# Attention: long products in half-bank pieces, one or two beside every block

## The chip, the cores and the metric

The kernel runs on one core of one Trainium2 chip. The metric is the device time of one execution in microseconds, the median of several runs. Engines are named as in the profile: PE (TensorE's matmuls) and PEld (its weight loads), DVE (VectorE), ACT (ScalarE), POOL (GpSimd), SP (the queue that issues most transfers).

## The reference

A layer of three parts on x of shape (8, 512, 512), all in float32:

```python
x = x + 0.5 * ffn(layernorm(x))      # 16 experts choose 256 tokens each; one shared expert matrix
x = x + attention(layernorm(x))
x = x + 0.5 * ffn(layernorm(x))
```

The attention is a differential one, and the change lies in it. For each of 16 heads (4 groups of keys and values, head width 32) there are two causal softmax maps, and the second is taken away from the first with a factor; the difference goes through a softmax of its own:

```python
q = rope((x @ Wq).reshape(b, s, H, 2 * D))
k = rope((x @ Wk).reshape(b, s, KVH, 2 * D))
v = (x @ Wv).reshape(b, s, KVH, D)
scores = softmax(where(causal, NEG, energy) / sqrt(D))
diff = softmax(where(causal, NEG, scores[:, 0] - lam * scores[:, 1]))
att = einsum("bhqv,bvhd->bqhd", diff, v)
att = att * rsqrt(mean(att * att, -1) + EPS) * rms_w * (1 - LAM_INIT)
return att.reshape(b, s, E) @ Wo
```

## The kernel before

The order of the instructions is written out by hand. The first feed-forward part runs over the 8 batches, then attention, then the second feed-forward part.

**Blocks.** Attention is a list of 176 blocks, 22 for each batch. A batch has two phases (`gp` 0 and 1: two of the four key groups each), so there are 16 phases of 11 blocks. A phase goes over the four query tiles `i` of 128 queries: one block for tile 0, two for tile 1, four each for tiles 2 and 3, the later tiles with more keys. The main loop takes one block `k` further in each turn, and in the same turn works on earlier blocks, so that every engine has a stage of a different block:

- PE: transposes of the probabilities of block k-3 (`turn_pe`, L882), attention sums of block k-4 (`values_pe`, L913), short products, and the scores of the next block (`scores`, L761), which go into PSUM banks 0 to 3;
- DVE: the reciprocals of block k-1 (L799), then the "first subtraction" of block k (`energies`, L777: mask and minimum, 4, 8 or 16 operations that read banks 0 to 3), then the slot "mid", copies of the transposes (L898) and of the attention sum (L926), the slot "dve", and the difference of the two maps of block k-1 (L848);
- ACT: exponentials of an earlier block's difference (L862), exponentials of block k (L790), the slots "act first", "act mid" and "act", copies of the transposes (L900);
- POOL: masks (L828), factors and weights (L804, L814), and the slot "pool".

**Work in slots.** What belongs to no block stands beside blocks, in named slots filled by a table: `rope_steps` (a projection of q or k, L635, its two rotation products on DVE, L654 and L656, two transfers on SP's queue that swap neighbouring rows, and a sum on POOL, L665), `value_steps` (L610), `norm_steps` (statistics on DVE, normalising on POOL, transposes on PE, L582, and a copy to `hT` on ACT, L589) and `finish_steps` (the normalisation of the attention sum, with short products L694, L700 and L715, a multiplication L723, the output projection L731 and the residual L737). There are ten projections of q and k, four output projections and one of the values in each batch. In a phase's turns from 0 to 10 the projections stand at (0, 0, 1, 2, 3) or (0, 1, 1, 2, 4), each as a whole: four products of 512 columns into one PSUM bank, two of the products in the slot "long" and two in "long 2".

**The next scores.** A table says where the scores of the next block stand in the turn: ahead of "long" (0), between "long" and "long 2" (1), or behind both (2):

```python
PLACES = (1, 0, 1, 2, 2, 0, 0, 0, 0, 0, 2, 0, 0, 0, 0, 0, 0, 0, 0, 0, 0, 0)
```

**Banks.** PSUM has eight banks of 512 float32 columns. Banks 0 to 3 hold scores, 4 and 5 the transposes. Banks 6 and 7 (`MISC`) are taken in turn by everything else, long or short: projections, attention sums, transposes of the normalised x, the products of `finish_steps`. A tile is waited for by the tile that takes its bank next.

Of the kernel before, what the change touches and what calls it, by code (L numbers as in the profile page):

```python
# [23 lines left out]
Q = P // 2  # L24
NEXP = 16
# [16 lines left out]
def macaron_kernel(  # L42
# [80 lines left out]
    turns = {}  # L123

    def bank(of, name, shape=(P, S)):

        n = turns[of] = turns.get(of, -1) + 1
        return banks.tile(list(shape), F32, name=name, tag=f"b{of[n % len(of)]}")
# [414 lines left out]
    def attention(f0, f1, home, first_end, projections_end, drain):  # L543
        QSCALE = -1.0 / float(D) ** 0.5

        def misc(name):
            return bank(MISC, name)


        def norm_steps(at, b, st):  # L550

            mv = tiny.tile([P, TPB, 2], F32, name=f"mv{b}", tag="a_mv", bufs=1)
            rstd = tiny.tile([P, TPB], F32, name=f"rstd{b}", tag="a_rstd", bufs=1)
            nmr = tiny.tile([P, TPB], F32, name=f"nmr{b}", tag="a_nmr", bufs=1)
            hs, ps = {}, {}

            def stats(i):
                s6 = tiny.tile([P, 6], F32, name=f"s6_{b}_{i}", tag="a_s6")
                nc.vector.bn_stats(s6, x_sb[b][:, i, :])
                nc.vector.bn_aggr(mv[:, i, :], s6)  # L560

            def scale():
                nc.scalar.activation(rstd, mv[:, :, 1], AF.Ln, bias=ln_eps)
                nc.scalar.activation(rstd, rstd, AF.Exp, scale=-0.5)

            def shift():
                nc.vector.scalar_tensor_tensor(
                    nmr, mv[:, :, 0], -1.0, rstd, ALU.mult, ALU.mult
                )

            def apply(i):
                where, tag = home["h"]
                hs[i] = where.tile([P, E], F32, name=f"h{b}_{i}", tag=tag, bufs=2)
                return nc.gpsimd.tensor_scalar(
                    hs[i], x_sb[b][:, i, :], rstd[:, i : i + 1], nmr[:, i : i + 1],
                    ALU.mult, ALU.add,
                )

            def turn(i):
                ps[i] = misc(f"htp{b}_{i}")  # L580
                for c in range(EC):
                    nc.tensor.transpose(  # L582
                        ps[i][:, c * P : (c + 1) * P], hs[i][:, c * P : (c + 1) * P], ident
                    )

            def put(i):
                if i == 0:
                    st["hT"] = home["hT"].tile([P, EC, S], F32, name=f"hT{b}", tag="hT")
                nc.scalar.copy(  # L589
                    st["hT"][:, :, i * P : (i + 1) * P],  # L590
                    ps[i].rearrange("p (c t) -> p c t", c=EC),
                )

            for i in range(TPB):
                at((0, 0, 3, 3)[i], "dve", lambda i=i: stats(i))
                at((6, 6, 8, 9)[i], "pool", lambda i=i: apply(i))
                at((7, 8, 9, 10)[i], "short", lambda i=i: turn(i))
                at((7, 8, 9, 10)[i], "act mid", lambda i=i: put(i))
            at(3, "act", scale)
            at(4, "mid", shift)  # L600

        def value_steps(at, o, b, st):
            t = {}

            def pe(h):
                if h == 0:
                    t["ps"] = misc(f"vps{b}")
                for i in (2 * h, 2 * h + 1):
                    for c in range(EC):
                        nc.tensor.matmul(  # L610
                            t["ps"][:, i * P : (i + 1) * P],
                            st["hT"][:, c, i * P : (i + 1) * P], wv_sb[:, c, :],
                            start=(c == 0), stop=(c == EC - 1),
                        )

            def act():
                st["v"] = home["v"].tile([P, TPB, KVH * D], F32, name=f"v{b}", tag="v", bufs=2)
                nc.scalar.copy(st["v"].rearrange("p i d -> p (i d)"), t["ps"])

            at(o, "long", lambda: pe(0))  # L620
            at(o, "long 2", lambda: pe(1))
            at(o + 1, "act first", act)

        def rope_steps(at, o, b, gp, n, st):

            name = f"r{b}_{gp}_{n}"
            c0 = gp * P if n == 0 else (gp * R + n - 1) * P
            w = wk_sb if n == 0 else wq_sb
            t = {}

            def pe(h):
                if h == 0:
                    t["ps"] = misc(f"{name}_ps")
                for c in (2 * h, 2 * h + 1):
                    nc.tensor.matmul(  # L635
                        t["ps"], w[:, c, c0 : c0 + P], st["hT"][:, c, :],
                        start=(c == 0), stop=(c == EC - 1),
                    )

            def place():  # L640

                tiles, tag = st["kq"][gp], f"kq{gp}_"
                if n == 0:
                    tiles["k"] = home[f"kq{gp}"].tile([P, S], F32, name=name, tag=f"{tag}k")
                    return tiles["k"]
                h, r = divmod(n - 1, 2)
                if h == 0:
                    tiles[r] = home[f"kq{gp}"].tile([P, S, 2], F32, name=name, tag=f"{tag}{r}")
                return tiles[r][:, :, h]

            def dve():
                f = 1.0 if n == 0 else QSCALE
                out = t["out"] = place()
                nc.vector.scalar_tensor_tensor(out, t["ps"], f, cosk, ALU.mult, ALU.mult)  # L654
                by = home["by"].tile([P, S], F32, name=f"{name}_by", tag="by", bufs=2)
                nc.vector.scalar_tensor_tensor(by, t["ps"], -f, sink, ALU.mult, ALU.mult)  # L656

                t["sw"] = home["sw"].tile([P, S], F32, name=f"{name}_sw", tag="sw", bufs=2)
# [8 lines left out]
            at(o, "long", lambda: pe(0))  # L667
            at(o, "long 2", lambda: pe(1))
            at(o + 1, "mid", dve)
            at(o + 2, "pool", pool)  # L670

        def finish_steps(at, os, b, i, st):
# [4 lines left out]
            def square():  # L677
                t["sq"] = home["sq"].tile([P, 4, P], F32, name=f"{name}_sq", tag="sq", bufs=2)
# [10 lines left out]
            def sums():  # L689


                t["ss"] = misc(f"{name}_ss")
# [17 lines left out]
            def turn():  # L710

                t["f"] = misc(f"{name}_f")
                for c in range(4):
                    for q in range(4):
                        nc.tensor.matmul(  # L715
                            t["f"][q * D : (q + 1) * D, c * P : (c + 1) * P],
# [4 lines left out]
            def norm():  # L721
                t["an"] = home["sq"].tile([P, 4, P], F32, name=f"{name}_an", tag="sq", bufs=2)
                nc.vector.tensor_tensor(  # L723
                    t["an"], st["aT"][i], t["f"].rearrange("p (c q) -> p c q", c=4), ALU.mult
                )
# [13 lines left out]
            o0, o1, o2, o3, o4 = os  # L739
            at(o0, "act", square)  # L740
            at(o1, "short", sums)
            at(o1, "act mid", root)
            at(o3, "short", turn)
            at(o3, "dve", norm)
            at(o4, "long", lambda: pe(0))
            at(o4, "long 2", lambda: pe(1))
            at(o4 + 1, "mid", residual)
# [154 lines left out]
        def values_pe(u):  # L902
# [3 lines left out]
            av = misc(f"av{u['id']}")  # L906
            u["av"] = av
# [77 lines left out]

        def plan(ph):
# [3 lines left out]
            if gp == 0:  # L990
                if b < B:
                    for n, o in enumerate((0, 0, 1, 2, 3)):
                        rope_steps(at, o, b, 1, n, sts[b])
                    if b + 1 < B:
                        sts[b + 1] = new_batch()
                        norm_steps(at, b + 1, sts[b + 1])
                if b > 0:
                    finish_steps(at, (0, 1, 2, 4, 5) if b < B else LAST[0], b - 1, 2, sts[b - 1])
                    finish_steps(at, (3, 5, 5, 7, 8) if b < B else LAST[1], b - 1, 3, sts[b - 1])
            else:  # L1000
                if b + 1 < B:
                    for n, o in enumerate((0, 1, 1, 2, 4)):
                        rope_steps(at, o, b + 1, 0, n, sts[b + 1])
                    value_steps(at, 3, b + 1, sts[b + 1])
                finish_steps(at, (4, 5, 5, 7, 9), b, 0, sts[b])
                finish_steps(at, (6, 7, 7, 9, 10), b, 1, sts[b])
                if b == B - 1:
                    for n, os in enumerate(EARLY):
                        early_steps(at, n, *os)

# [25 lines left out]
        order = ("short", "long", "long 2", "act mid", "mid", "dve", "act", "pool")  # L1036
        pre = placer(-20)
        norm_steps(pre, 0, sts[0])
        for n in range(R + 1):
            rope_steps(pre, 12 + n, 0, 0, n, sts[0])  # L1040
# [15 lines left out]
        value_steps(placer(-2), 0, 0, sts[0])  # L1056
# [11 lines left out]
        for k in range(K + 13):  # L1068
            u = blocks[k] if k < K else None
            u1, uE, u2, u3 = (blocks[k - d] if 0 <= k - d < K else None for d in (1, 2, 3, 4))  # L1070
            if k in starts:
                ph = starts.index(k)
                if ph == 2 * B - 1:
# [23 lines left out]
            place = PLACES[k % len(PLACES)]  # L1097
# [94 lines left out]
    for i in range(TPB):  # L1192
# [5 lines left out]
        hT=proj, kq0=proj, by=proj, sw=proj, h=(proj, "sw")  # L1198
# [3 lines left out]
    def first_end():  # L1202
        first_y.close()
        opened["out"], opened["blocks"] = pool("out", "right"), pool("blocks", "right")
        home.update(aT=opened["out"], sq=opened["out"], h=(opened["out"], "sq"))
# [51 lines left out]

    attention(f0, f1, home, first_end, projections_end, drain)
# [13 lines left out]
    for name in ("late", "out", "early"):  # L1272
        opened[name].close()

# [68 lines left out]
```

## Time and profile before

| what | before |
|---|---|
| median of 3 runs | 1421.35 us (1421.13 to 1421.44) |
| profiled execution, first to last instruction | 1420.2 us |
| mean granted clock of TensorE | 0.969 |
| busy: PE, DVE, ACT, POOL | 1328.5, 1154.9, 1047.0, 685.4 us |
| one batch of attention, in the steady part | 129.6 us |
| projections of q (L635, wq) | 512 passes of 601 ns |
| first subtraction (L777) | 1024 operations of 453 ns |
| rotation (L654, L656) | 80 each, 690 and 681 ns |
| swap transfers | 160 of 128 KB, 2.0 us to landing |

The page's first part gives the busy time of each engine and its share of the span, the second the same in 40 slices of 35.5 us, in tenths. A matmul in float32 stands in the trace as two passes. A group's mean is the length of one instruction; instructions that follow each other on an engine overlap by a part of it, so that their spacing is shorter than their length.

### The profile page before, as it was taken

How to read it: one execution, taken by the hardware profiler on the slowest of the kernel's cores; microseconds unless marked ns; L12 is line 12 of the kernel's file. 1: busy time of each engine (PE TensorE's matmuls, PEld its weight loads, DVE VectorE, ACT ScalarE, POOL GpSimd, SP SyncE). 2: the span in 40 equal slices, each digit the busy share in tenths (PEclk: the TensorE clock that was granted, in tenths of full speed). 3: DMA queues.
4: the chain of work that ended last, by engine and by line, in shares of the span. 5: the costliest groups of instructions: out<-in, count | busy, mean ns of one | idle time of the engine just before them, and what ended most of it. 6: DMA issues, size and time to landing. Idle time of an engine off the chain costs nothing.

```text
span 1420.2 us, 30675 instructions
## 1 busy us (share of the span) xinstructions
PE 1328.5 (94%) x9774; PEld 738.4 (52%) x9774; DVE 1154.9 (81%) x4405; ACT 1047.0 (74%) x3644; POOL 685.4 (48%) x1314
## 2 busy tenths in 40 slices
PE   6999899899999999999999999999999997998998
PEld 4544444455555555555555555555455555555443
DVE  6554769899989988998999899889989989654566
ACT  3411128999899898989898998989899989844110
POOL 5433626554555455454545555554545555443230
PEclk9999988999999999999999999999999997999999
DMA  9300011000000101000000001010000001000006
GB/s 344 91 1 0 0 38 38 9 31 24 16 24 17 39 1 38 9 31 9 32 24 16 28 13 39 2 38 16 24 13 27 28 13 40 1 5 1 1 1 236
DMA packets 27554, 48.19 MB, mean 34 GB/s; under 512 B 4720, under 2 KB 6016, under 8 KB 27392
## 3 DMA queue, kind: packets, MB, share of 16 engines
q1 hardware_dynamic: 25152, 42.03, 8.3%
q10 hardware_dynamic: 2208, 4.19, 0.8%
q8 instruction: 77, 1.26, 0.4%
q14 instruction: 85, 0.70, 0.2%
q0 software_dynamic: 32, 0.01, 0.0%
HBM read 16.86 MB, written 8.39 MB: 18 GB/s over the span
## 4 chain that ended last, share of the span: by engine, by line
PE 60%; ACT 13%; DVE 10%; issue 2%; POOL 0%; ACTq 0%; DVEq 0%
PE r_ps L635 18%; PE sc L761 8%; PE f_o L731 8%; ACT e L790 7%; PE tp L882 6%; PE yps L381 6%; PE av L913 4%; DVE e L777 4%; DVE t L848 3%; ACT t L862 2%; PE vps L610 2%; PE kps L403 2%; PE f_f L715 1%; ACT eT L900 1%; PE tp L325 1%
## 5 line engine op out<-in xcount | busy, mean ns | idle before, releaser
L790 ACT ACTIVATE e<-e,nb 128x192 f32<-128x192 f32 (+7 forms) x1024 | 535.5, 532 | 6.5 <-DVE nb L777 4.3
L777 DVE CUSTOM_DVE_ANT_0 e<-sc,mpos 128x192 f32<-128x192 f32 (+7 forms) x1024 | 400.8, 453 | 23.7 <-PE sc L761 16.5
L814 POOL TENSOR_SCALAR e<-e,z 128x512 f32<-128x512 f32 (+7 forms) x512 | 295.9, 590 | 16.7
L862 ACT ACTIVATE t<-t,nm 128x512 f32<-128x512 f32 (+7 forms) x512 | 270.0, 534 | 42.2 <-DVE nm L848 42.0
L761 PE MATMUL sc<-r,r 32*128 32x64 f32 (+7 forms) x2048 | 245.3, 456 | 10.8 <-DVE nb L777 4.9
L848 DVE CUSTOM_DVE_ANT_0 t<-e,z 128x512 f32<-128x512 f32 (+7 forms) x512 | 240.6, 518 | 5.1 <-POOL e L814 4.2
L635 PE MATMUL r_ps<-hT,wq_sb 128*128 128x512 f32 x512 | 235.6, 601 | 0.1
L381 PE MATMUL yps<-we,y 128*128 128x512 f32 x456 | 216.5, 612 | 1.0 <-ACT y L388 0.7
L882 PEld LDWEIGHTS tp<-ident,t 128*128 128x128 f32 x1280 | 146.5, 144 | 135.6 <-ACT eT L900 43.3
L882 PE MATMUL tp<-ident,t 128*128 128x128 f32 x1280 | 188.6, 283 | 28.1 <-ACT eT L900 26.6
L790 ACT ACTIVATION_READ_ACCUMULATOR e<-e,nb 128x1 f32 x1024 | 202.1, 197 | 0.0
L665 POOL TENSOR_TENSOR r<-r,r_sw 128x512 f32<-128x512 f32 x80 | 103.0, 1296 | 175.8 <-DVE z L799 84.2
L761 PEld LDWEIGHTS sc<-r,r 32*128 32x128 f32 x2048 | 117.4, 188 | 90.7 <-DVE nb L777 44.6
L391 POOL TENSOR_TENSOR y<-y,eb 128x512 f32<-128x512 f32 x57 | 73.1, 1283 | 164.4 <-ACT y L388 134.3
L635 PEld LDWEIGHTS r_ps<-hT,wq_sb 128*128 128x128 f32 x512 | 93.0, 190 | 113.9 <-issue 99.6
L388 ACT COPY y<-yps 128x512 f32<-128x512 f32 x57 | 33.4, 586 | 155.6 <-PE yps L381 155.6
L828 POOL TENSOR_SCALAR_AFFINE_SELECT e<-e 128x128 f32<-128x128 f32 x256 | 79.2, 316 | 99.4 <-ACT e L790 99.4
L898 DVE COPY eT<-tp 128x512 f32<-128x512 f32 (+1 forms) x176 | 112.0, 636 | 16.6 <-PE tp L882 16.6
L381 PEld LDWEIGHTS yps<-we,y 128*128 128x128 f32 x456 | 81.3, 192 | 78.4 <-issue 73.6
L731 PE MATMUL f_o<-wo_sb,f_an 128*128 128x512 f32 x256 | 118.6, 605 | 0.0
L804 POOL TENSOR_TENSOR z<-z,over 128x4 f32<-128x4 f32 (+1 forms) x192 | 38.0, 201 | 142.6 <-DVE z L799 142.5
L862 ACT ACTIVATION_READ_ACCUMULATOR t<-t,nm 128x1 f32 x512 | 100.4, 196 | 0.0
(123 smaller groups left out, 1668.6 us busy)
## 6 DMA issues: line engine op xcount, KB each, us to landing
r_sw<-r_by SPq DMA_DIRECT2D x160, 128.0 KB, 2.0
x<-in_x_dram SPq DMA_DIRECT2D x6, 1024.0 KB, 13.2
out_dram<-x SPq DMA_DIRECT2D x6, 512.0 KB, 3.2
out_dram<-x ACTq DMA_DIRECT2D x6, 512.0 KB, 3.2
x<-in_x_dram SPq DMA_DIRECT2D x8, 256.0 KB, 8.2
we<-in_expert_w_dram SPq DMA_DIRECT2D x2, 1024.0 KB, 7.7
wq_sb<-in_wq_dram SPq DMA_DIRECT2D x1, 2048.0 KB, 13.9
wo_sb<-in_wo_dram SPq DMA_DIRECT2D x8, 128.0 KB, 2.8
```

The source lines that it names most:

```text
L381: nc.tensor.matmul(held["yps"], buf[b][:, i, c * P : (c + 1) * P], held["we"][:, c, :], start=(c == 0), stop=(c == EC - 1),)
L635: nc.tensor.matmul(t["ps"], w[:, c, c0 : c0 + P], st["hT"][:, c, :], start=(c == 0), stop=(c == EC - 1),)
L665: return nc.gpsimd.tensor_add(t["out"], t["out"], t["sw"])
L731: nc.tensor.matmul(t["o"], t["an"][:, c, :], wo_sb[:, c // 2, c % 2, :], start=(c == 0), stop=(c == 3),)
L761: nc.tensor.matmul(u["sc"][j][:, part.cols], q[j * D : (j + 1) * D, q0 : q0 + P], kq["k"][j * D : (j + 1) * D, : part.n], start=True, stop ...
L777: nc.vector.tensor_tensor_reduce(out=u["e"][:, j, part.cols], in0=u["sc"][j][:, part.cols], in1=mpos[:, S - part.n :], scale=1.0, scalar=3 ...
L790: nc.scalar.activation(e, e, AF.Exp, bias=u["nb"][:, c : c + 1], scale=-1.0, accum_out=u["z"][:, 0, c : c + 1],)
L814: nc.gpsimd.tensor_scalar(e, e, u["z"][:, 1, c : c + 1], u["z"][:, 0, c - nr : c - nr + 1], ALU.mult, ALU.mult,)
L848: u["diff"] = nc.vector.tensor_tensor_reduce(out=u["t"][:, par, r * w : r * w + part.n], in0=u["e"][:, 2 * par, s], in1=u["e"][:, 2 * par ...
L862: nc.scalar.activation(t, t, AF.Exp, bias=u["nm"][:, par, r : r + 1], scale=-1.0, accum_out=z2[:, col : col + 1],)
L882: nc.tensor.transpose(u["tp"][par][:, o : o + P], u["t"][:, par, (r * (i + 1) + c) * P : (r * (i + 1) + c + 1) * P], ident,)
L898: nc.vector.tensor_copy(o, s)
```

## The change

Four things are changed in attention, for phases 0 to 14 and for what stands ahead of the first block; the last phase (15) keeps the tables and whole banks of before.

- Every long product is made in two pieces of 256 columns (half a bank): projections by halves of the tokens, output projections by halves of the columns, values by pairs of tiles. What reads them is split likewise: rotation, swap, sum, residual, copy.
- New tables put one or two pieces beside nearly every block: the first of a turn in "long", a second one in "long 2". `hT` is in two tiles, and its transposes come in halves too, spread over turns 3 to 10.
- Banks 6 and 7 are held for the whole time as two tiles of halves: halves 0 and 1 (bank 6) for the pieces, halves 2 and 3 (bank 7) for short results. `LONG[second]` gives a first piece half 0 and a second piece half 1.
- The scores of the next block always stand between "long" and "long 2".

The instructions that read and write, and their sums, are otherwise as before. The diff, cut to its core:

```diff
+    def half_bank(n, name):
+        if n // 2 not in duo:
+            duo[n // 2] = duo["pool"].tile([P, S], F32, name=f"half{n // 2}", tag=f"b{6 + n // 2}")
+        return duo[n // 2][:, n % 2 * W : (n % 2 + 1) * W]
...
+        LONG = (0, 1)
+        WHOLE = 2 * B - 1
...
+        def piece(at, o, second, pe, slot, read):
+
+            at(o, "long 2" if second else "long", lambda: pe(LONG[second]))
+            at(o + 1, slot, read)
...
-            def pe(h):
-                if h == 0:
-                    t["ps"] = misc(f"{name}_ps")
-                for c in (2 * h, 2 * h + 1):
+            def pe(m):
+                t["ps"] = half_bank(m, f"{name}_ps")
+                for c in range(EC):
                     nc.tensor.matmul(
-                        t["ps"], w[:, c, c0 : c0 + P], st["hT"][:, c, :],
+                        t["ps"], w[:, c, c0 : c0 + P], st["hT"][half][:, c, :],
                         start=(c == 0), stop=(c == EC - 1),
                     )
...
-                nc.vector.scalar_tensor_tensor(out, t["ps"], f, cosk, ALU.mult, ALU.mult)
-                by = home["by"].tile([P, S], F32, name=f"{name}_by", tag="by", bufs=2)
-                nc.vector.scalar_tensor_tensor(by, t["ps"], -f, sink, ALU.mult, ALU.mult)
-
-                t["sw"] = home["sw"].tile([P, S], F32, name=f"{name}_sw", tag="sw", bufs=2)
+                nc.vector.scalar_tensor_tensor(out, t["ps"], f, cosk[:, ts], ALU.mult, ALU.mult)
+                by = home["by"].tile([P, W], F32, name=f"{name}_by", tag="by", bufs=3)
+                nc.vector.scalar_tensor_tensor(by, t["ps"], -f, sink[:, ts], ALU.mult, ALU.mult)
+
+                t["sw"] = home["sw"].tile([P, W], F32, name=f"{name}_sw", tag="sw", bufs=4)
...
-            at(o, "long", lambda: pe(0))
-            at(o, "long 2", lambda: pe(1))
-            at(o + 1, "mid", dve)
+            piece(at, o, second, pe, "mid", dve)
             at(o + 2, "pool", pool)
...
-            av = misc(f"av{u['id']}")
-            u["av"] = av
+            name = f"av{u['id']}"
+            av = u["av"] = misc(name) if duo["whole"] else half_bank(2, name)
...
+        ROPES = [
+            [(0, 0, 0), (0, 1, 0), (1, 0, 0), (1, 1, 0), (2, 0, 0),
+             (2, 1, 1), (3, 0, 1), (4, 0, 1), (5, 0, 1), (6, 0, 1)],
+            [(0, 0, 0), (0, 1, 0), (1, 0, 0), (1, 1, 0), (2, 0, 0),
+             (3, 0, 1), (4, 0, 1), (5, 0, 1), (6, 0, 1), (7, 0, 1)],
+        ]
+        VALUES = ((2, 1), (3, 1))
+        NORM = (
+            (0, 0, 1, 1), 1, (2, 4, 7, 8),
+            ((0, 0, 3, 3), (0, 1, 4, 3), (1, 0, 5, 3), (1, 1, 6, 3),
+             (2, 0, 8, 3), (2, 1, 9, 2), (3, 0, 9, 3), (3, 1, 10, 3)),
+        )
+        FINISH = (
+            (4, (5, 2), 7, ((8, 0), (9, 0))),
+            (7, (8, 3), 9, ((10, 0), (10, 1))),
+            (0, (1, 3), 2, ((7, 0), (8, 0))),
+            (3, (5, 2), 7, ((9, 0), (9, 1))),
+        )
...
-            place = PLACES[k % len(PLACES)]
+            place = PLACES[k % len(PLACES)] if duo["whole"] else 1
```

A triple of `ROPES` is the turn, whether the piece is the turn's second, and which half of the tokens it takes; a pair of `VALUES` is the turn and whether it is the second. `FINISH` has the turns of the square, the sums (with their half), the transposition and the two pieces of the output projection.

## The prediction

> **What bounds the kernel now.** I read the page first, parts 1 and 2. No engine has much room, and the attention stage, slices 6 to 35, is dense on all three of PE, DVE and ACT.
>
> ```profile
> PE 1328.5 (94%) x9774; PEld 738.4 (52%) x9774; DVE 1154.9 (81%) x4405; ACT 1047.0 (74%) x3644; POOL 685.4 (48%) x1314
> ...
> PE   6999899899999999999999999999999997998998
> ...
> DVE  6554769899989988998999899889989989654566
> ACT  3411128999899898989898998989899989844110
> ```
>
> The stage repeats: one batch takes 129.6 us. So I asked for the busy time in windows over one batch, cut where VectorE starts the first subtraction (L777) of a block. The columns after the window are its length and then the busy us of PE, PEld, DVE, ACT and POOL, with PE's granted clock behind them.
>
> ```profile
> 719.40:741.80 22.40, 22.40 (x156) 12.03 (x155) 21.05 (x111) 20.93 (x95) 9.76 (x27) 1.00 0.07 25
> 741.80:785.10 43.30, 40.05 (x384) 22.77 (x383) 40.07 (x136) 39.10 (x124) 26.15 (x50) 1.00 0.05 20
> 785.10:807.80 22.70, 22.11 (x121) 11.59 (x122) 18.92 (x106) 21.75 (x97) 9.69 (x27) 0.92 0.07 25
> 807.80:849.00 41.20, 38.69 (x415) 23.61 (x414) 37.55 (x129) 38.06 (x122) 23.09 (x46) 1.00 0.06 21
> ```
>
> Windows 1 and 3 hold the three blocks with query tiles 0 and 1, where most long products now stand; windows 2 and 4 hold eight blocks each, of query tiles 2 and 3. DVE is busy 117.6 us of 129.6 and ACT 119.8. PE's 123 us flatters it, since pipelined matmuls overlap in that row. What unevenness costs is bounded by DVE's 12.0 idle us in a batch.
>
> Then the chain that ended last, asked for one stretch (start, us, what). It shows what happens where a long product stands ahead of the next scores:
>
> ```profile
> 745.43 3.63 PE r_ps L635 x8
> 749.06 0.89 PE sc L761 x8
> 749.96 0.15 DVE e L777
> ...
> 751.46 0.47 DVE e L777
> 751.93 0.01 DVE nb L777
> 751.94 0.60 DVE r L654
> 752.54 0.61 DVE r_by L656
> 753.15 0.04 issue
> 753.19 1.08 PE f_f L715 x32
> ```
>
> A projection, then the scores, then VectorE's four subtractions, then the two readings of the projection's bank, and only 0.04 us later a PE instruction that had waited for that bank. That is the whole ring that the change closes; before, it occurs a few times in a batch. The two waits on it stand at the line's end, first in VectorE's timeline, then in PE's:
>
> ```profile
> 749.94 0.56 DVE L777 CUSTOM_DVE_ANT_0 e<-sc,mpos 128x384 f32<-128x384 f32 x1 [0.83 <-PE sc L761]
> ```
>
> ```profile
> 753.19 1.08 PE L715 MATMUL f_f<-f_r,ident 128*32 128x128 f32 x32 [1.66 <-DVE r_by L656]
> ```
>
> **The change, part by part.** *PE's work.* A batch has 14 long products of 512 columns and they become 28 pieces, with the values' two halves 30. The chain gives 3.63 us for 8 passes of 512 columns, so a piece of 8 passes of 256 costs about 1.81 us and the two together what one cost. The spread moves 3.6 us lumps out of the six small blocks; that is what is to be gained.
>
> *VectorE's work.* Per batch 10 projections (two operations each), 4 residuals and 4 norms are split: 28 operations more. A copy out of PSUM takes 684 ns at 512 columns (L898) and 420 ns at 256 (L926); with some 0.08 us of overlap from one operation to the next (0.60 us apart in the chain, 0.69 long in the timeline) a half costs 0.34, so a split costs 0.08: 2.2 us a batch, all on VectorE's queue. ScalarE's splits (four of hT, one of v) cost under 0.3 us a batch.
>
> *DMAs.* The 20 swaps of a batch become 40 of half the size on SP's queue, which carries nothing else here; they land in 2.0 us and the sum on GpSimd comes a block later, so I count nothing. Without that cover, one late landing is 2 us at the head of a half batch. GpSimd's sums (L665, 1296 ns) become two of about 0.65 each; it is busy about half of the time, nothing.
>
> *The bank.* This is the part that decides. In the built program a first piece always takes half 0 and a second half 1 of the same bank, and the wait of each block's first piece names the last reader of the bank, whichever half that read. That reader stands in VectorE's queue in the "mid" slot of the same block, behind all the subtractions of the block. The next scores now stand behind the first piece in every block. So the ring closes each time: piece, scores(k+1), subtractions(k+1), readings, piece. Queued behind the waiting piece on PE are the next scores, and VectorE's next round, and ScalarE's exponentials behind that.
>
> Its length for the 16 large blocks, mean of widths 320, 384, 448 and 512: piece 1.81; scores until the first subtraction about 1.00 (0.89 plus 0.07 in the chain at 384; 0.75 for 320 and about 1.1 for 512 at the ends); four subtractions 2.04 (their spacing is 0.48 at 384 in the timeline, 0.61 at 512, 0.41 at 320); two half readings 0.68 and 0.08 to the end of the last; 0.05 to PE. Sum 5.66 us. VectorE's own round in these blocks is (40.07 + 37.55) / 16 = 4.85 us plus a tenth for splits, so the ring is longer by about 0.7 and VectorE waits for scores. 16 x 5.66 = 90.6 us, where windows 2 and 4 take 84.5: +6.1. Corrections go both ways: four blocks read a residual of one operation (4 x 0.34 less), one has two pieces to read (0.68 more), and in three PE itself, with two pieces and the short products ahead, is later than the ring by up to 1 us. From -1 to +2 together; I take 0.
>
> The six small blocks: the ring there is 6.6 to 7.3 us (eight or sixteen subtractions of 2.2 to 2.9, four readings), against 45.1 / 6 = 7.5 now, of which VectorE fills 6.7 and ScalarE 7.1. Losing the 3.6 us lumps could give back 1.4 us; ScalarE, 21.75 of 22.70 in window 3, and the moved statistics could cost 1. I take 0.
>
> So 129.6 becomes 135.7: +6.1 a batch, bounds +3.7 and +9. Phases 0 to 14 of 16 have the new form, 165 of 176 blocks: 7.5 batches, +46 us (28 to 68).
>
> *Ahead of the blocks.* Five projections run back to back with two banks (181.26 to 200.34 on PE). Now each waits for the four half readings of the one before: about 1.5 us four times, +6 us, bounds 0 and 9, as the updates of x fit into VectorE's time beside.
>
> *Elsewhere* the last phase and the final stage keep whole banks: 0.
>
> The sum: the profiled span is 1420.2 us, 1.15 under the median; 1420.2 + 46 + 6 = 1472.2, and with 1.15 around it 1473.
>
> Two rules of the Trainium skill stand beside this, and the sum does without both. "PSUM — Partial Sum Buffer", section on bank collisions, says to guard PSUM by bank and quadrant, not by address: it speaks against taking halves as separate buffers, and no run yet shows more than the built waits. If halves could be guarded singly, only blocks with two pieces would be released one reading sooner, 0.7 us in one large block, and the sum would be about 1468. "TensorE: Matmul & The Clock Gate", section on the HAM clock gate, lets the clock fall after an idle window of some 3.4 us; the trace differs: window 3 has 0.92, and in the 3.4 us ahead of its drop PE is busy 3.04 us. By the rule the changed kernel, which spreads PE's work, would lose no clock (about 1.8 us a batch less, 1460); by the row thin work is enough and the loss stays, as I take it.
>
> **Rivals.** *Levelling wins (faster).* If the ring were hidden, the idle of 12.0 us could halve: 117.6 + 2.2 + 6 = 125.8, -3.8 a batch, -28 in all, +6 ahead: 1399 us. For it speaks that PE's blocks run from one lump of long products to none, and that DVE fills windows 1 and 2 to 93% already. It decides from the point where what VectorE does between the readings and the next subtractions exceeds piece, scores and signals, 2.94 us; in the large blocks that is 4.85 + 0.1 - 2.04 - 0.7 = 2.2. It would need 0.75 us more work per block, or scores that do not wait. The waits shown above at 749.94 and 753.19 speak against it.
>
> *The ring and more (slower still).* Short results share one bank as well, so VectorE's copy of the attention sum (L926) waits for ScalarE's copy of the transposed half in the same bank, which stands behind the exponentials. With up to 0.5 us in half the large blocks, PE's late pieces and another clock drop of 1.8 us: +12 a batch, 90 in all, 9 ahead: 1520 us.
>
> *The halves act as buffers after all*: if the waits that I read are met long before in practice, about 1430 us, the loss only in splits (2.2 x 7.5 = 16) against some of the idle.
>
> **How the numbers follow.** The forecast, 1440 to 1497, has 0.63; slower still 0.17; 1424 to 1440 0.09; faster 0.09; no change that a measurement of this kernel can tell (0.2%, 2.8 us) 0.02. The range 1438 to 1512 leaves out levelling below and the worst of the second rival above. Faster 0.09, same 0.02, slower 0.89.
>
> **What would show it.** In the changed profile: VectorE's first subtraction waiting for the scores' line in most large blocks, 0.5 to 1 us each, and PE's piece waiting for the second reading of the projection; windows of a batch of 135 to 137 us, with the growth in the large blocks; VectorE's busy time up by about 2 us a batch and its idle by about 4; pieces of 8 passes at 1.8 us. I am wrong if the large blocks come in under 5.3 us each, if PE waits on ScalarE rather than on the readings, or if the small blocks gain several us.

## The result, and the profile after

The changed kernel takes 1521.29 us (median of 4 runs, 1516.48 to 1522.04), where the kernel before takes 1421.39 beside it: 1.0691 times as long, 95% interval 1.0674 to 1.0708. The direction was as predicted; the loss, 99.9 us, is nearly twice the predicted 52 and lies 9 us above the range. The profiled execution is 1519.3 us long. Laid against the one before by the first subtractions of its blocks, it says where the 99.1 us went:

| stretch | before | after | difference | predicted |
|---|---|---|---|---|
| ahead of the first block | 207.6 | 214.4 | +6.8 | +6 |
| phase 0 (11 blocks) | 57.6 | 66.1 | +8.5 | +3 |
| phases 1 to 14, 7 batches | 908.6 | 992.7 | +84.1, 12.0 a batch | +43, 6.1 a batch |
| the rest | 246.4 | 246.1 | -0.3 | 0 |

The page first, its parts 1 and 2:

```profile
PE 1306.7 (86%) x10638; PEld 861.9 (57%) x10638; DVE 1159.9 (76%) x4621; ACT 1058.6 (70%) x3684; POOL 695.1 (46%) x1394
...
PE   6999778888888888888888888888888887899898
...
DVE  6545668888888887888788888878888889754566
ACT  4311138978888888888888988888888888954210
```

In slices 6 to 35, PE, DVE and ACT had 8 and 9 before; now all three have mostly 8. PE, DVE and ACT have hardly more to do (their busy times change by -21.8, +5.0 and +11.6 us); they wait more. The weight loads (PEld) grow by 123.5 us, as there are 10638 instead of 9774 of them; the kernel with the splits alone, below, has as many (10670, 915.4 us) and loses 8 us. Then the batch in four windows, cut as before at the first subtraction of a block (length, then the busy us of PE, PEld, DVE, ACT and POOL, then the granted clock):

```profile
776.70:800.40 23.70, 19.57 (x201) 15.28 (x201) 22.28 (x120) 22.07 (x99) 8.75 (x26) 1.00 0.07 24
800.40:848.00 47.60, 41.93 (x401) 28.71 (x402) 39.52 (x139) 39.14 (x124) 27.05 (x54) 1.00 0.06 18
848.00:868.40 20.40, 16.53 (x130) 12.05 (x128) 17.74 (x108) 20.40 (x95) 10.76 (x28) 1.00 0.08 27
868.40:917.80 49.40, 41.88 (x457) 29.57 (x457) 38.96 (x140) 39.83 (x126) 23.34 (x51) 1.00 0.05 18
```

The sixteen large blocks (windows 2 and 4) take 97.0 us instead of 84.5; the six small ones 44.1 instead of 45.1. DVE's idle time in a batch rises from 12.0 to 22.6 us. PE's clock is 1.00 in all four. It is not so in every batch: in the window that follows, 917.70 to 941.40, it is 0.96.

The chain, for one block of window 4 (start, us, what), is the predicted ring, closed:

```profile
885.14 1.99 PE half L672 x8
887.14 0.89 PE sc L826 x8
888.03 0.15 DVE e L842
...
890.26 0.43 DVE r_by L694
890.69 0.04 issue
890.73 1.99 PE half L672 x8
```

Piece, scores, subtractions, two readings, the next piece: 5.59 us for a block of width 384, and the next block starts the same way. Last, VectorE's waits and PE's over the seven batches (waiting line, releasing line, us in all, times, longest):

```profile
DVE e L842 <- PE sc L826: 95.6, 121, 1.8
DVE r L692 <- ACT v L655: 22.3, 14, 1.7
DVE aT L991 <- ACT hT L616: 17.6, 30, 0.7
DVE aT L991 <- ACT f_r L742: 12.0, 14, 2.0
```

```profile
PE half L672 <- DVE r_by L694: 83.8, 77, 3.1
PE half L802 <- DVE x L808: 28.2, 28, 1.9
```

The first line of VectorE and both of PE are the ring. The subtractions wait for the scores in 121 of the 154 blocks of these batches, in 107 of the 112 large ones. Lines 2 to 4 are something else: VectorE stands still until ScalarE has read *another* half of the same bank. Line 2 shows it for bank 6 (a projection in one half, the values in the other), lines 3 and 4 for bank 7 (the attention sum beside a transposed half, or beside the sums of a finish). Together 51.9 us in seven batches; in the same stretch of the kernel before, the copy of the attention sum waits for no copy of ScalarE's.

### The profile page after: what moved, and what is told of

Same layout as the page of the kernel before. It is cut to its first block, busy times and chain, and to the rows that moved or that the text cites. A ratio compares the mean times of both kernels' runs of the same rounds, so it can differ in the third digit from the quotient of the medians.

```text
span 1519.3 us, 33264 instructions
## 1 busy us (share of the span) xinstructions
PE 1306.7 (86%) x10638; PEld 861.9 (57%) x10638; DVE 1159.9 (76%) x4621; ACT 1058.6 (70%) x3684; POOL 695.1 (46%) x1394
## 4 chain that ended last, share of the span: by engine, by line
PE 37%; ACT 23%; DVE 19%; issue 5%; POOL 1%; DVEq 0%; ACTq 0%
ACT e L855 15%; DVE e L842 10%; PE half L672 10%; PE sc L826 7%; PE half L802 6%; PE yps L402 6%; ACT t L927 5%; DVE t L913 2%; DVE r_by L694 2%; PE kps L424 2%; DVE r L692 1%; ACT eT L965 1%; PE tp L947 1%; PE f_o L770 1%; DVE nb L842 1%
## 5 line engine op out<-in xcount | busy, mean ns | idle before, releaser
L672 PE MATMUL half<-hT,wq_sb 128*128 128x256 f32 x1024 | 260.3, 399 | 95.1 <-DVE r_by L694 95.1
L703 POOL TENSOR_TENSOR r<-r,r_sw 128x256 f32<-128x256 f32 x160 | 117.0, 742 | 368.8 <-DVE z L864 279.2
L672 PEld LDWEIGHTS half<-hT,wq_sb 128*128 128x128 f32 x1024 | 188.1, 193 | 149.8 <-DVE r_by L694 109.2
L826 PE MATMUL sc<-r,r 32*128 32x64 f32 (+7 forms) x2048 | 197.5, 454 | 3.9 <-DVE nb L842 2.4
L855 ACT ACTIVATION_READ_ACCUMULATOR e<-e,nb 128x1 f32 x1024 | 192.6, 188 | 0.0
L947 PE MATMUL tp<-ident,t 128*128 128x128 f32 x1280 | 180.2, 281 | 8.9 <-ACT eT L965 8.8
L802 PE MATMUL half<-wo_sb,f_an 128*128 128x256 f32 x448 | 111.7, 392 | 45.0 <-DVE x L808 28.2
L826 PEld LDWEIGHTS sc<-r,r 32*128 32x128 f32 x2048 | 87.4, 188 | 71.1 <-issue 51.6
L802 PEld LDWEIGHTS half<-wo_sb,f_an 128*128 128x128 f32 x448 | 80.5, 189 | 70.2 <-DVE x L808 35.4
L692 DVE SCALAR_TENSOR_TENSOR r<-half,cst 128x256 f32<-128x256 f32 x160 | 67.2, 420 | 41.3 <-ACT v L655 22.3
```

The lines of the kernel that those rows point to most:

```text
L672: nc.tensor.matmul(t["ps"], w[:, c, c0 : c0 + P], st["hT"][half][:, c, :], start=(c == 0), stop=(c == EC - 1),)
L703: return nc.gpsimd.tensor_add(t["out"], t["out"], t["sw"])
L802: nc.tensor.matmul(t["o", h], t["an"][:, c, :], wo_sb[:, c // 2, c % 2, es], start=(c == 0), stop=(c == 3),)
L826: nc.tensor.matmul(u["sc"][j][:, part.cols], q[j * D : (j + 1) * D, q0 : q0 + P], kq["k"][j * D : (j + 1) * D, : part.n], start=True, stop ...
L855: nc.scalar.activation(e, e, AF.Exp, bias=u["nb"][:, c : c + 1], scale=-1.0, accum_out=u["z"][:, 0, c : c + 1],)
L947: nc.tensor.transpose(u["tp"][par][:, o : o + P], u["t"][:, par, (r * (i + 1) + c) * P : (r * (i + 1) + c + 1) * P], ident,)
```

## The experiments

Four theories stood against each other. *Theory 1*: the ring costs it. *Theory 2*: the waits of VectorE on ScalarE in shared banks cost it. *Theory 3*: the splits cost it. *Theory 4*: the place of the scores behind a long product costs it, whatever guards the banks. Ratios are to the kernel before on the same chip.

**Theory 4 alone: the place of the scores.** In the kernel before:

```diff
-            place = PLACES[k % len(PLACES)]
+            place = PLACES[k % len(PLACES)] if k >= starts[2 * B - 1] else 1
```

> The kernel before, with the next scores issued behind the first long step in every block of phases 0 to 14, as the change has it; long products stay whole, in whole banks used in turn. Theory 1, the ring needs both the scores behind the piece and the guard of one bank: here a product waits only for the reading of the one before the last, so the time moves little, 1421 to 1440 us. Theory 4, the scores behind a long product are enough: a product of 3.6 us, or its first half of 1.8, stands ahead of them in every block with one, about 14 in a batch, and 0.5 to 1.0 us each is lost, 50 to 100 us in all, 1470 to 1520.

1424.64 us, ratio 1.0019 (1.0007 to 1.0031). With whole banks in turn the place costs next to nothing. Theory 4 falls.

**Theory 3 alone: the splits.** In the kernel before, pieces of half the columns and all that reads them in two, without the new tables and half banks; the values and the transposes stay whole. One of its edits:

```diff
-                nc.vector.scalar_tensor_tensor(out, t["ps"], f, cosk, ALU.mult, ALU.mult)
+                for h in range(2):
+                    ts = slice(h * W, (h + 1) * W)
+                    ps = t["ps"][:, ts]
+                    nc.vector.scalar_tensor_tensor(out[:, ts], ps, f, cosk[:, ts], ALU.mult, ALU.mult)
```

> The kernel before, with its tables and its places of the scores, but every projection and every residual as two pieces of 256 columns in the two halves of one whole bank, and its readings, swaps, GpSimd sums and the norm's product in two as well; whole banks are still used in turn, and the values and transposed halves are as before. Theory 1 says that the splits are cheap: 28 more VectorE operations a batch at 0.07 us, 2 us a batch on its queue, part of it in idle time, 1424 to 1442 us. Theory 3, splits are dear (SP's and GpSimd's instructions doubled, more issue on PE): 1455 or more.

1430.51 us, ratio 1.0058 (1.0039 to 1.0077): 8 us. VectorE's busy time rises from 1154.9 to 1169.1 us, near the 16 that the prediction put on its queue; the time grows by about half of that. As the main cause theory 3 falls.

**The ring cut: scores ahead of the piece.** In the changed kernel:

```diff
-            place = PLACES[k % len(PLACES)] if duo["whole"] else 1
+            place = PLACES[k % len(PLACES)] if duo["whole"] else 0
```

> The changed kernel with the next block's scores issued ahead of the first piece in every block of phases 0 to 14, instead of behind it; the halves, their order and all waits on them stay. Theory 1, the ring (piece, scores, subtractions, readings, piece) sets the blocks: with the scores out of it, VectorE's first subtraction no longer waits for PE, the 105.6 us of that wait fall under 30, the large blocks of a batch come back from 97.0 us to 84 to 88, and the time to 1425 to 1450 us. Theory 2, the waits of VectorE on ScalarE's copies in the shared banks carry about half of the loss by themselves: those waits stay as they are and the time is 1465 to 1485. Theory 3, the splits are dear: 1500 or more, since nothing is merged.

1464.6 us, ratio 1.0300 (1.0281 to 1.0319): 56 of the 99 us are gone, with all splits, halves and guards in place. (Its six runs spread from 1455.4 to 1466.7: two at 1455 with a mean granted clock of 0.953 and 0.959, four above 1463 with 0.948 to 0.951. The profile is of one at 1455.7.) VectorE's waits in its seven batches:

```profile
DVE r L692 <- ACT v L655: 25.3, 14, 2.3
DVE aT L991 <- ACT hT L616: 22.2, 30, 1.2
DVE r L692 <- PE half L672: 15.6, 15, 2.1
DVE aT L991 <- ACT f_r L742: 13.8, 14, 2.2
...
DVE e L842 <- PE sc L826: 0.5, 2, 0.3
```

The wait for the scores falls from 95.6 to 0.5 us, so the ring is real; the three waits on ScalarE stay and even grow, and 41 us of loss stay with them. Not all of the 41 need be theirs: VectorE now also waits 15.6 us for late pieces (2.2 after the change), and PE's clock over these batches is 0.96, where it was 0.99. In the block from 756.62 to 763.63, for one, the clock is 0.64, and VectorE then waits 1.53 us for a piece. The time is at the lower end of what theory 2 gave and above all that theory 1 gave: both seem to be at work.

**The ring cut at its other end: readings ahead of the subtractions.** In the changed kernel:

```diff
+            fill(k, "head")
             if u is not None:
                 energies(u, (0,))
...
-            piece(at, o, second, pe, "mid", dve)
+            piece(at, o, second, pe, "head", dve)
```

> The changed kernel with VectorE's readings of the pieces (rotation and residual) issued at the head of the block, ahead of the subtractions, instead of behind them; the scores stay behind the first piece. Theory 1, the ring: the piece's wait now ends before the subtractions, so the ring is cut at its other end; the wait of the projection on the second reading (98.4 us) falls under 30 and the time to 1425 to 1455 us, although the subtractions start 0.7 us later in their round. Theory 4, the place of the scores behind the piece is what costs, whatever guards the halves: no change, 1505 to 1525. Theory 2, waits on ScalarE in the shared banks: VectorE's rotation, now ahead, waits longer for ScalarE's copy of the values, and the time stays over 1480.

1523.19 us, ratio 1.0700 (1.0676 to 1.0725): no gain, as theory 4 had said and for another reason. First PE's timeline where two pieces stand in a block, then VectorE's:

```profile
886.48 0.93 PE L826 MATMUL sc<-r,r 32*128 32x384 f32 x8
887.34 2.05 PE L644 MATMUL half<-wv_sb,hT 128*128 128x128 f32 x16
...
893.63 2.91 PE L672 MATMUL half<-hT,wq_sb 128*128 128x256 f32 x8 [2.78 <-ACT v L655]
```

```profile
889.50 0.42 DVE L692 SCALAR_TENSOR_TENSOR r<-half,cst 128x256 f32<-128x256 f32 x1 [3.67 <-PE half L644]
```

The reading of the first half stands until the *second* piece, in the other half of the bank and behind the scores, is done (889.4), and PE's next piece until ScalarE has copied the values from that half. So, as this program guards it, the bank is one resource in both directions: a write waits for the readings ahead of it, and a reading waits for the writes ahead of it, whichever half they touch. Where one piece stands alone the cut works: five successive blocks of window 4 (from 320 to 512 wide) take 25.1 us instead of 29.1. What they gain the blocks with two pieces lose; as a test of theory 1 it is inconclusive by its time.

**ScalarE's copies ahead of its exponentials.** In the changed kernel, phases 0 to 14:

```diff
+            if not duo["whole"]:
+                fill(k, "act mid")
             if uE is not None:
                 exps2(uE)
             if u is not None:
                 exps(u)
             fill(k, "act mid")
```

> The changed kernel with ScalarE's copies out of the shared banks (values, transposed halves, root of the finish) issued ahead of both sets of exponentials in phases 0 to 14, instead of behind them. Theory 2, these copies stand late and VectorE's readings of the same bank wait for them: the waits of the rotation on the values' copy (22.3 us) and of the attention sum's copy on the transposed half and the root (32.1 us) fall under 10 together, and the time by 25 to 55 us, to 1465 to 1495. Theory 1, the ring alone: VectorE's waits move to the scores and the time stays within 10 us, 1510 to 1525. A loss is possible where ScalarE, now waiting for PE's short products at the head, starts the exponentials late: up to 1540.

1603.9 us, ratio 1.1274 (1.1257 to 1.1291), far beyond the loss I had allowed for. ScalarE's waits over its seven batches say why:

```profile
ACT hT L616 <- PE half L605: 98.3, 36, 5.2
ACT f_r L742 <- PE half L735: 54.4, 22, 3.5
```

The head of ScalarE's queue now waits for products that PE makes late in the block, and the exponentials stand behind that. It moves a wait to an engine that is as full as VectorE, and says nothing on theory 2.

**The copy of the values alone ahead**, in the changed kernel and in the one with the scores ahead:

```diff
+            fill(k, "act first")
             if uE is not None:
                 exps2(uE)
```

> The changed kernel with ScalarE's copy of the values alone issued ahead of both sets of exponentials; what it copies was made a block earlier, so it has nothing to wait for. Theory 2, the readings of the rotation that wait for this copy in the same bank cost their 1.74 and 1.47 us in two blocks of a batch: 15 to 27 us less than the changed kernel's 1521, 1494 to 1506. Theory 1, the ring alone: VectorE, released sooner, waits for the scores instead in the next blocks, and the time falls by under 10, 1511 to 1521.

> The changed kernel with the scores ahead of the first piece and ScalarE's copy of the values ahead of the exponentials, both. With the ring gone (1464.6 us), the two longest idle times of VectorE in a batch are those ahead of rotations that wait for the values' copy, 2.33 and 1.47 us. Theory 2: they go, 3 us a batch over 7 batches, 1436 to 1450 us. If another wait takes their place (the late pieces of PE, ScalarE's transposed halves): 1455 to 1466.

1523.17 us, ratio 1.0714 (1.0696 to 1.0732), and 1470.45, ratio 1.0346 (1.0322 to 1.0370): nothing gained in either. In the first, VectorE's wait on the values' copy falls from 22.3 to 7.6 us, but its reciprocal now waits 30.5 us for exponentials, where it waited 11.6. ScalarE's timeline shows the reason; these are the two values' pieces of one batch:

```profile
874.82 0.37 ACT L655 COPY v<-half 128x256 f32<-128x256 f32 x1 [2.77 <-PE half L644]
...
881.50 0.37 ACT L655 COPY v<-half 128x256 f32<-128x256 f32 x1 [1.90 <-PE half L644]
```

My expectation that this copy had nothing to wait for was wrong: PE finishes the second piece late, and the exponentials now stand behind the copy. In PE's timeline of these blocks, piece, scores, values' piece, transposes and attention sum follow each other without a wait, 6.6 us from 870.05 to 876.63 and 6.2 from there to 882.86. Here PE itself is now the bound, and the wait on ScalarE hid little beyond it: the two blocks take 13.6 us instead of 14.3, and the run as a whole gains nothing. This part of theory 2 falls.

**The copy of the attention sum behind the differences.** In the changed kernel alone, and with the scores ahead:

```diff
-            if u3 is not None and u3["last"]:
+            if u3 is not None and u3["last"] and duo["whole"]:
                 values_out(u3)
             fill(k, "dve")
             if u1 is not None:
                 difference(u1)
+            if u3 is not None and u3["last"] and not duo["whole"]:
+                values_out(u3)
```

> The changed kernel with one thing moved: VectorE's copy of the attention sum behind the differences of the block. The scores stay behind the first piece, the values' copy where it was. If the ring (theory 1) and the wait of this copy on ScalarE (theory 2) are two causes that add, it gains what it gained without the ring, 60 to 70 us: 1452 to 1465. If the ring is the longer chain and covers it: VectorE's 4.8 us a batch ahead of this copy turn into waits for the scores, and 1495 to 1515. If the waits on ScalarE are the cause and the ring only follows from them: below 1440.

> The changed kernel with the scores ahead of the first piece and the copy of the attention sum behind the differences; the values' copy behind the exponentials, as the change has it. With the values' copy ahead as well it took 1404.8 us, and that part by itself lost 2 to 6 us in both other pairs: 1397 to 1405. If the rotation's waits for the values' copy come back at their 2.33 and 1.47 us: 1415 to 1430.

Alone 1494.52 us, ratio 1.0509 (1.0494 to 1.0525); with the scores ahead 1407.23, ratio 0.9894 (0.9879 to 0.9909), faster than the kernel before. VectorE's waits over seven batches, alone and then together:

```profile
DVE e L842 <- PE sc L826: 100.4, 114, 1.2
...
DVE aT L991 <- ACT hT L616: 7.4, 6, 1.2
```

```profile
DVE r L692 <- ACT v L655: 28.7, 14, 2.8
...
DVE aT L991 <- ACT hT L616: 10.9, 12, 1.5
...
DVE e L842 <- PE sc L826: 0.9, 6, 0.2
```

Alone, the 29.6 us in which the sum's copy waits for ScalarE fall to 7.4, and the waits for the scores rise from 95.6 to 100.4, so that some 5 of the 22 us come back there. With the ring cut, the sum's waits fall from 36.0 to 11.2, and the scores' are 0.9; the reciprocal's wait for exponentials grows by 6.8. The four ratios make a table:

| | sum's copy ahead of the differences | behind them | gain |
|---|---|---|---|
| scores behind the piece | 1.0691 | 1.0509 | 26 us |
| scores ahead | 1.0300 | 0.9894 | 58 us |
| gain | 56 us | 87 us | 113 us together |

(Gains are differences of ratios times 1421.4.) Either move alone gains some 32 us less than it does beside the other. That one wait hides behind the other is only in part shown. The sum's own waits shrink by nearly as much in either row (22.2 us and 24.8). What else shrinks in the second row are VectorE's waits for late pieces, from 15.6 to 1.9 us, and the loss of clock: over phases 1 to 14 it is 0.96 with the scores ahead alone and 0.99 with both moves (0.99 after the change, 1.00 with the late copy alone). By these means some 37 us of PE's full speed are missing in 930.3 us, and some 9 in 885.6 (estimates), so that up to 28 of the 58 us can be the clock. Whether the waits brought the clock down was not tested.

The same, with the values' copy ahead as a third move:

> The kernel with scores ahead of the piece and the values' copy ahead of the exponentials, and besides with VectorE's copy of the attention sum issued behind the differences of the block, instead of ahead of them, so that it need not stand still for ScalarE's copy of a transposed half or root in the same bank. Theory 2: the 0.7 us ahead of this copy in some five blocks of a batch go, 2 to 3.5 us a batch, 15 to 25 us less than without it, 1415 to 1435 us. If PE's next short product, which waits for the same bank, becomes late instead: no gain or a loss of up to 20 us.

1404.78 us, ratio 0.9885 (0.9861 to 0.9908), the same within the intervals as without the third move.

**The control: the late copy in the kernel before.** The same edit as above, in phases 0 to 14 of the kernel before.

> The kernel before with its copy of the attention sum behind the differences in phases 0 to 14. Whole banks in turn do not tie this copy to ScalarE's (its idle time is 0.2 us in two blocks of a batch), so there is little to gain: 1415 to 1424 us if theory 2 is a matter of the shared bank. If the late copy is a gain by itself, whatever the banks: 1395 or less, and the late copy, not the shared bank, would explain the 60 us. Or a loss of up to 15, where the next product waits for the bank longer.

1435.66 us, ratio 1.0096 (1.0079 to 1.0113): a loss of 13.6 us, at the far end of what was allowed. ScalarE's squares wait 21.2 us for this copy in its seven batches, 2.1 before. So the late copy is no gain by itself; it gained in the kernel where ScalarE's reading of the same bank stands in its way.

**Ahead of the first block.** The kernel of 1407.2 us, with first and second pieces in two banks until the first block starts:

```diff
-            at(o, "long 2" if second else "long", lambda: pe(LONG[second]))
+            at(o, "long 2" if second else "long", lambda: pe((0, 2)[second] if early else LONG[second]))
```

> The changed kernel with the scores ahead of the piece and the late copy of the attention sum, and the projections ahead of the first block in halves of two banks instead of one, so that a piece waits for two half readings of the projection before, not for four. The 6.7 us that the stage ahead of the first block grew by came from these waits: 3 to 6 us less than the same kernel without this part. If they came from the doubled swaps or sums: no change within 1.5 us.

1401.75 us, ratio 0.9856 (0.9841 to 0.9871), the best of all, 1.4% faster than the kernel before. The first subtraction comes at 207.2 us instead of 213.6 (207.6 in the kernel before), so the 6.8 us ahead of the blocks were waits for the readings of one bank.

## Why the prediction was right in direction and short in size

*The ring, right.* Its place and its members were as predicted, its wait stands in most blocks, though not in each (121 of 154), and cutting it took away its wait. Its length was short by 0.1 us: its terms give 5.50 at width 384, and 5.59 came. The term that was off is the piece with the scores behind it: 885.14 to the subtraction at 888.03 is 2.89 us, where 1.81 and 0.96 were counted. The piece is 1.99 us long here; 1.81 was half of a product in full flow. At 0.1 us for each of 16 blocks, the large blocks would be 92.2 instead of the predicted 90.6 (an estimate).

*The corrections, wrong.* The step that failed is "From -1 to +2 together; I take 0". The large blocks took 97.0 us, 6.4 more than predicted. Of that the ring's own length is 1.6, so the corrections came to +4.8. The largest term is "PE itself ... is later than the ring by up to 1 us", in three blocks. These are the blocks with two pieces between their scores and the next. The first subtractions of one of them and of the two blocks behind it:

```profile
875.59 0.56 DVE L842 CUSTOM_DVE_ANT_0 e<-sc,mpos 128x384 f32<-128x384 f32 x1 [0.48 <-PE sc L826]
882.69 0.49 DVE L842 CUSTOM_DVE_ANT_0 e<-sc,mpos 128x320 f32<-128x320 f32 x1 [0.92 <-PE sc L826]
888.01 0.56 DVE L842 CUSTOM_DVE_ANT_0 e<-sc,mpos 128x384 f32<-128x384 f32 x1 [1.16 <-PE sc L826]
```

The two with a values' piece take 7.2 us (from 868.39) and 7.1 (from 875.59). The third, from 800.43 to 807.22, takes 6.8, and in it PE works without a wait. Blocks of the same widths (320, 384, 320) with one piece take 5.3, 5.7 and 5.3 us. That is 1.4 to 1.9 us more each, 4.8 together, of which 0.7 went when the values' copy stood ahead. The second term is the class that I had only as a rival, readings of one bank by two engines. With the late copy alone, the large blocks of this batch take 96.0 us instead of 97.0, and the small ones 42.8 instead of 44.1 (one of them 7.97 instead of 9.44). Against these two terms stand the four blocks that read a residual, -1.4 as counted. Together they come to 4.4 of the 4.8. Over the whole kernel this order among readers is worth 26 us with the ring in place, and it stood in the sum at nothing. Without it the kernel takes 1494.5 us, inside the range that was given: of the 48 us by which 1473 fell short, some 27 are this term, and some 21 the late pieces, the longer ring and what stands below.

*The rival "the ring and more", right in its number.* It named the copy of the attention sum waiting for ScalarE, and gave +12 a batch and 1520 us; 12.0 and 1521 were measured. Both waits stood in the same built order, and the sum had only one of them; 0.17 was too low a chance for the other. Its terms are only in part of the size that it gave them. The drop of the clock is absent in the batch shown, but not in the next: there PE waits 3.09 us for the readings, the clock is 0.76 from 935.90 to 943.10, the piece takes 3.09 us instead of 1.99, and the batch from 848.03 to 990.73 takes 142.7 us, where the one before took 141.1. Four of the seven batches are of this kind. Late pieces cost more than it had. So its exact agreement is in part luck.

*"Levelling wins", right behind the two waits.* It put a batch at 125.8 us and the kernel at 1399. With both waits moved out of the way, a batch takes 126.5 us, and the kernel 1407.2, or 1401.8 with two banks ahead. With both waits gone the spread of long products over the blocks is worth about what this rival promised.

*The rest.* Ahead of the blocks: +6 predicted, +6.8 measured. Splits: 16 us on VectorE's queue predicted, 14.2 of busy time and 8 of time measured alone. Small blocks: -1.0, inside the bounds. Phase 0 grew by 8.5, not 3; with both moves it falls back by 6.0, so most of it has the same two causes, and I did not follow the rest. The clock: I kept window 3's loss by the row of the trace before; after, that window is at 1.00 with PE busy for 16.53 of 20.40 us, so my reading that thin work is enough to bring the clock down did not hold there. After the change PE waits 3.06 to 3.10 us ahead of one piece in six of the seven batches; behind four of these waits (to 512.29, 654.99, 938.72 and 1081.41) the clock falls, behind two (to 371.22 and 797.65) it stays at 1.00. Over the seven batches the clock is 0.99, where it was 0.98, so part of the 1.8 us a batch that I left in the sum may have been gained, by these means some 1.2 (an estimate).

*The rule on banks.* The Trainium skill, "PSUM — Partial Sum Buffer", section on bank collisions, says that ScalarE and VectorE reading the same bank at once collide as well, also at columns that have nothing in common, and that a guard must go by bank and quadrant. My sum had used it for PE's writes against VectorE's readings only. The waits of VectorE on ScalarE's copies (51.9 us in seven batches) show the guard between two readers; what happens without it was not tried.

*Open.* Halves in banks of their own, which would leave the order as it is and take the guard away, were not tried: six of the eight banks hold scores and transposed maps.

## What to carry to other kernels

In this program the two halves of a PSUM bank acted as one buffer: before sharing one, write down for each half who writes it, who reads it and where in that engine's queue the reading stands, and price every pair, two readers included. When two waits lie in one block, remove both before judging either: here each alone seemed worth 26 or 56 us, and together they were worth 113. A copy that may have to wait for another engine belongs behind the work that need not wait, but only there: the same move cost 14 us where nothing stood in its way.

## What the runs showed of the hardware

In the changed kernel eight float32 passes of 256 columns took 1.99 us after a wait, with the next product starting 1.93 us after them (885.14 and 890.73), and 1.83 us after them at 800.33, where they followed other products at once; eight of 512 in full flow took 3.63. VectorE's split reading took 0.33 to 0.34 us for each half where the whole took 0.60, so a split costs 0.07. The mean granted clock of the profiled executions ranged from 0.948 to 0.985, from kernel to kernel without a relation to the time (0.985 at 1494 us, 0.973 at 1405); within the runs of one kernel, the one with the scores ahead, the slower ones had the lower clock. I have no explanation for the differences between kernels.
